# Causal mask matmuls on 64 by 64 tiles of the array: two heads in the rows, two halves of the keys in the columns

## The chip, the core and the metric

The kernel runs on one core of a Trainium2 chip. A core has a matrix engine (TensorE, in the profile PE for matmuls and PEld for weight loads), a vector engine (DVE), a scalar engine (ACT), GpSimd (POOL) and queues that start DMAs (SP among them). Matmuls read their operands from SBUF and write to PSUM[...]. The engines run side by side and wait for one another through semaphores.

The metric is device time in microseconds. Before the change it is 3176.01 us, the median of 3 runs (3175.93 to 3178.2).

## What is computed

A pre-norm block on x of shape 8 x 1024 x 512: an attention whose queries, keys and values are sines and cosines of the normalised input, and then a mixture of eight experts. What matters here is the causal attention:

```python
B, S, D = x.shape                       # 8, 1024, 512
H, dh = w_q.shape                       # 16, 32
...
Q = jnp.concatenate([cos_q, sin_q], axis=-1)      # 64 per head
...
K = jnp.concatenate([cos_k, sin_k], axis=-1)
...
V = cos_v + sin_v
scores = jnp.einsum('bqhd,bkhd->bhqk', Q, K) / scale
causal = jnp.triu(jnp.ones((S, S), dtype=bool), k=1)
scores = jnp.where(causal, -jnp.inf, scores)
attn = jax.nn.softmax(scores, axis=-1)
out = jnp.einsum('bhqk,bkhd->bqhd', attn, V).reshape(B, S, D)
```

A head's queries and keys have 64 elements each, so a product of them needs only half of the array's 128 rows.

## The kernel before

The attention stage goes through 32 steps (`n` in the main loop; 8 sequences times 4 groups of four heads). A step has two pairs of heads, and each pair two halves `h` of the queries (512 each): 128 passes of score tiles in all. The generator `scores` makes the tiles of one pass one after another, with keys in the partitions and queries in the columns. The two heads of a pair, `a` = 0 and 1, lie in partitions 0 to 63 and 64 to 127 of `pair` and so in the upper and lower 64 rows of the array, and they write to two banks of PSUM (`ps[:, a, ...]`). The score matmuls (L684, fp32) take a stationary operand of 64 rows by 128 keys, which the profile writes as "64*128". An fp32 matmul shows up as two passes, each with its own weight load, so that a score tile of 512 queries for two heads makes four rows in the trace.

Tiles in which no key is later than a query need no mask. In each pass three tiles hold the diagonal: one of 512 queries (a first block of 128 keys), one that puts two blocks of keys side by side (384 and 128 queries), and one of 256. There `scores` adds a large negative number to the scores of later keys, by matmuls in bf16 that accumulate into the same PSUM (L698). Their rows are not elements of a query but 64 keys of a half block: the stationary operand `keys_b` holds identity blocks, and the moving operand `later_b` holds 0 or the negative number for each of the 64 keys and each of up to 128 queries. `part` is the half of the 128 keys: half 0 needs only the first 64 queries, half 1 all 128. So a diagonal tile has four mask matmuls, two halves for two heads; in the tile with two key blocks, each covers both blocks in one instruction (128 and 256 columns instead of 64 and 128). Before the change `keys_b` has 128 columns for each half, of which the other half's 64 are zero, so that every mask matmul writes all 128 partitions of the tile and adds zero to the other half.

After its mask each tile goes to ACT, which takes the exponential of both heads at once (L704) out of PSUM into SBUF; three score tiles fit in PSUM (`ps_sc`, 3 buffers). `attend` then multiplies them with the values (AV, L718, fp32, stationary 128 keys by 64 columns, "128*64"), the two heads in the two halves of the columns. `by_halves` (L216) transposes with 64 rows by 128 columns. The router's matmuls (L858, L875) use tiles of 128 rows by 32 columns, the experts (L1238 and on) all of 128 by 128.

The order of the instructions on PE, ACT, DVE and SP is written by hand: the main loop (L1736 to L1899) advances the generators of scores, attention, transposes, layernorm and router in turn, and each engine carries out its instructions in that order. The stage ends where the last `attend` ends, and PE goes over to the experts. `mask` (L288), called once at the start (L1720), fills `later_b` and `keys_b` on POOL from the fp32 masks of `rest_of_loads`; L266 first clears `keys_b`.

Of the kernel before, what the change touches and what calls it, by code (L numbers as in the profile page):

```python
# [15 lines left out]
BF16 = mybir.dt.bfloat16  # L16
# [6 lines left out]
P = 128  # L23
# [51 lines left out]
def preln_attn_moe_kernel(  # L75
# [21 lines left out]
    nc = tc.nc  # L97
# [35 lines left out]
    own = to_router.pool("own", 1, **left)  # L133
# [48 lines left out]
    ident = own.tile([P, P], F32, name="ident")  # L182
# [26 lines left out]
    def two_banks():  # L209
        return ps_sc.tile([P, 2, 512], F32, name="ps_s")  # L210
# [40 lines left out]
    ps = two_banks()[:, 0, : 6 * NCH]  # L251
# [10 lines left out]
    before = own.tile([P, P], F32, name="before")  # L262


    keys_b = own.tile([P, 2, P], BF16, name="keys_b")
    nc.gpsimd.memset(keys_b, 0.0)  # L266
    later_b = own.tile([P, 2, P], BF16, name="later_b")
    e_row = own.tile([P, E], F32, name="e_row")
    e_row_low = own.tile([P, E], F32, name="e_row_low")
# [16 lines left out]
    later = row2.tile([P, NCH, 2 * P], F32, name="xT", bufs=1)[:, :3, :P]  # L286

    def mask():  # L288
        for part in range(2):
            for a in range(2):  # L290
                r = slice(a * 64, (a + 1) * 64)
                nc.gpsimd.tensor_copy(later_b[r, part, :], later[r, 1 + part - a, :])
                nc.gpsimd.tensor_copy(keys_b[r, part, part * 64 : part * 64 + 64], ident[r, r])

    def rest_of_loads():

# [367 lines left out]
    def tiles_of(h):  # L664


        def block(kb, at=0):
            q0 = max(512 * h, kb * P)
            return kb, q0, 512 * (h + 1) - q0, at

        d = 4 * h
        full = [[block(kb)] for kb in range(d + 1)]
        return full + [[block(d + 1), block(d + 3, 3 * P)], [block(d + 2)]]

    def scores(pair, h, es):

        for parts in tiles_of(h):
            n = sum(w for _, _, w, _ in parts)
            ps = two_banks()
            own_keys = parts[0][0] >= 4 * h  # L680
            for kb, q0, w, at in parts:
                for a in range(2):
                    r = slice(a * 64, (a + 1) * 64)
                    nc.tensor.matmul(  # L684
                        ps[:, a, at : at + w], lhsT=pair[r, 1, kb * P : (kb + 1) * P],
                        rhs=pair[r, 0, q0 : q0 + w], start=at == 0, stop=not own_keys,
                        skip_group_check=True,
                    )
            if own_keys:

                for part, w in ((0, 64), (1, P)):
                    for a in range(2):
                        r = slice(a * 64, (a + 1) * 64)
                        out_, late = ps[:, a, :w], later_b[r, part, :w]
                        if len(parts) == 2:
                            out_ = ps[:, a, :].rearrange("p (k q) -> p k q", q=P)[:, ::3, :w]
                            late = late.unsqueeze(1).to_broadcast([64, 2, w])
                        nc.tensor.matmul(  # L698
                            out_, lhsT=keys_b[r, part, :], rhs=late,
                            start=False, stop=part == 1, skip_group_check=True,  # L700
                        )

            e = ep.tile([P, 2, n], F32, name=f"e_{n}", bufs=8 if n == 512 else 2)
            nc.scalar.activation(  # L704
                e, ps[:, :, :n], AF.Exp, scale=UNIT * UNIT / math.sqrt(2 * DH)
            )
            es.append(e)
            yield
# [78 lines left out]
    def router(b):  # L787
# [163 lines left out]


        mask, prior = t3("mask"), t3("prior")
        TT(mask, hot[0], hot[1], ALU.add)
        nc.vector.memset(prior[:, 0, :], 0.0)
        for t in range(1, NTT):
            TT(prior[:, t, :], prior[:, t - 1, :], mask[:, t - 1, :], ALU.add)
        yield "places"
        place = one_bank()[:, : NTT * E]
        flat = lambda t: t.rearrange("p t e -> p (t e)")  # L960
        tokens_out(place, before, flat(mask), start=True, stop=False)
        tokens_out(place, ones, flat(prior), start=False, stop=True)
        place = place.rearrange("p (t e) -> p t e", e=E)
# [772 lines left out]
    for n in range(NCK):  # L1736
        more, late = n + 1 < NCK, last is not None
# [15 lines left out]
        if late:  # L1753
            products.insert(0, attend(n - 1, 1, 1, e11, halves1))
        ahead = [scores(pairs[0], h, es[h]) for h in range(2)]
        v_box = [None]
        asides = [keep(v_box, v_pre(n + 1))] if more else [first_rows]
# [94 lines left out]

        es, halves1 = [[], []], []
        ahead = [scores(pairs[1], h, es[h]) for h in range(2)]
        route_on(1)
        route_on(2)
# [103 lines left out]
```

## Time and profile before

| what | value |
|---|---|
| median of 3 runs | 3176.01 us (3175.93 to 3178.2) |
| the profiled execution, its own time | 3177.95 us |
| its span (first to last instruction) | 3176.2 us |
| mean granted clock of TensorE | 0.998 |
| mask matmuls L698: count, from, to | 1536, 36.4 us, 1251.3 us |
| their durations: 64, 128, 256 columns | 190, 217, 270 ns |
| exponentials L704 on ACT: count, busy, mean | 640, 569.4 us, 937 ns |
| casts of the masks on POOL (L292, L293), in all | 8, from 15.3 us to 17.3 us |

A row of the profile names a line of the kernel, an engine, an operation, what is written and read, and for a matmul the rows and columns of the stationary operand ("64*128") and the shape of the moving one ("64x512": 64 partitions, 512 columns). The duration of a matmul runs from its start until the end of its way through the array, which is modelled, so durations of matmuls that follow each other overlap. The time that one takes from the next is read from the distance of their starts.

### The profile page before, as it was taken

How to read it: one execution, taken by the hardware profiler on the slowest of the kernel's cores; microseconds unless marked ns; L12 is line 12 of the kernel's file. 1: busy time of each engine (PE TensorE's matmuls, PEld its weight loads, DVE VectorE, ACT ScalarE, POOL GpSimd, SP SyncE). 2: the span in 40 equal slices, each digit the busy share in tenths (PEclk: the TensorE clock that was granted, in tenths of full speed). 3: DMA queues.
4: the chain of work that ended last, by engine and by line, in shares of the span. 5: the costliest groups of instructions: out<-in, count | busy, mean ns of one | idle time of the engine just before them, and what ended most of it. 6: DMA issues, size and time to landing. Idle time of an engine off the chain costs nothing.

```text
span 3176.2 us, 52225 instructions
## 1 busy us (share of the span) xinstructions
PE 3112.0 (98%) x20086; PEld 2147.5 (68%) x20086; DVE 2303.7 (73%) x4808; ACT 1680.4 (53%) x2599; POOL 424.1 (13%) x387
## 2 busy tenths in 40 slices
PE   5999999999999999999999999999999999999998
PEld 2444444444444444689699699699698698698697
DVE  8888878887887775738658658658667767767765
ACT  7888888888888885413423423423423423423423
POOL 3000202020201122410110110110110110110010
PEclk9999999999999999999999999999999999999999
DMA  5535454555545352533523523523533433433421
GB/s 167 147 100 166 106 165 132 148 138 149 164 133 160 80 167 55 149 82 96 155 54 91 152 57 95 145 59 98 140 64 100 132 67 102 128 67 108 118 58 23
DMA packets 288552, 358.79 MB, mean 113 GB/s; under 512 B 28376, under 2 KB 199088, under 8 KB 276272
## 3 DMA queue, kind: packets, MB, share of 16 engines
q1 hardware_dynamic: 264944, 312.20, 33.7%
q0 software_dynamic: 22912, 43.22, 7.3%
q8 instruction: 160, 2.62, 0.4%
q14 instruction: 88, 0.72, 0.1%
q10 hardware_dynamic: 448, 0.02, 0.0%
HBM read 207.02 MB, written 81.22 MB: 91 GB/s over the span
## 4 chain that ended last, share of the span: by engine, by line
PE 78%; DVE 4%; ACT 1%; issue 1%; DMA 0%; SPq 0%; POOLq 0%; POOL 0%; DVEq 0%; ACTq 0%
PE ps_p L1238 30%; PE ps_p L1474 10%; PE ps_p L1537 10%; PE av L718 10%; PE ps_s L684 9%; PE ps_p L1352 8%; ACT e L704 1%; PE ps_s L216 1%; PE ps_s L698 1%; DVE qk_f L525 1%; DVE qk_r L448 0%; DMA qk<-qk_r 0%; DVE xT L838 0%; DVE xe L1174 0%; DVE xe_s L1186 0%
## 5 line engine op out<-in xcount | busy, mean ns | idle before, releaser
L704 ACT ACTIVATE e<-ps_s 128x1024 f32<-128x1024 f32 (+1 forms) x640 | 569.4, 937 | 183.5 <-PE ps_s L684 110.0
L684 PE MATMUL ps_s<-qk 64*128 64x512 f32 (+3 forms) x3072 | 598.3, 506 | 28.2 <-DMA qk<-qk_r 12.4
L718 PE MATMUL av<-e,v 128*64 128x512 f32 (+3 forms) x3072 | 523.4, 490 | 0.0
L684 PEld LDWEIGHTS ps_s<-qk 64*128 64x128 f32 x3072 | 262.3, 188 | 216.0 <-issue 106.9
L718 PEld LDWEIGHTS av<-e,v 128*64 128x64 f32 x3072 | 200.5, 137 | 283.0 <-issue 267.0
L1238 PE MATMUL ps_p<-xe,w 128*128 128x256 f32 (+1 forms) x1024 | 317.6, 433 | 1.1 <-issue 1.1
L1238 PE MATMUL ps_p<-xe_s,t 128*128 128x256 f32 (+1 forms) x1024 | 317.6, 433 | 0.0
L1238 PE MATMUL ps_p<-xe,t 128*128 128x256 f32 (+1 forms) x1024 | 317.6, 433 | 0.0
L1316 POOL DMA_INDIRECT out_dram<-y,slots x80 | 127.8, 1597 | 1261.3 <-ACT y L1311 1017.8
L769 POOL DMA_INDIRECT slot_d<-token,slot x128 | 156.6, 1223 | 997.3 <-issue 620.8
L1238 PEld LDWEIGHTS ps_p<-xe_s,t 128*128 128x128 f32 x1024 | 194.4, 190 | 81.4 <-issue 0.8
L1238 PEld LDWEIGHTS ps_p<-xe,t 128*128 128x128 f32 x1024 | 194.2, 190 | 80.4 <-issue 0.4
L1238 PEld LDWEIGHTS ps_p<-xe,w 128*128 128x128 f32 x1024 | 193.7, 190 | 79.4 <-issue 1.2
L1281 DVE TENSOR_TENSOR hid<-hid 128x256 f32<-128x256 f32 (+1 forms) x128 | 63.9, 499 | 206.4 <-ACT hid L1279 206.4
L1537 PE MATMUL ps_p<-w_t,hid 128*128 128x256 f32 x960 | 212.4, 379 | 0.8 <-DVE y L1590 0.8
L1537 PEld LDWEIGHTS ps_p<-w_t,hid 128*128 128x128 f32 x960 | 180.0, 190 | 24.4 <-DVE y L1590 1.2
L1238 PE MATMUL ps_p<-xe_s,w 128*128 128x256 f32 (+1 forms) x512 | 158.9, 433 | 0.6 <-ACT p L1254 0.6
L1352 PE MATMUL ps_p<-w,hid 128*128 128x256 f32 x640 | 142.9, 379 | 0.0
L1474 PE MATMUL ps_p<-w,hid 128*128 128x128 f32 x1104 | 141.8, 275 | 0.0
L698 PEld LDWEIGHTS <-keys_b 64*128 64x128 bf16 x1536 | 80.9, 95 | 89.7 <-issue 71.8
L1311 ACT ACTIVATE y<-y,slots 128x256 f32<-128x256 f32 (+1 forms) x120 | 65.9, 578 | 142.8 <-DVE y L1389 105.5
L1474 PEld LDWEIGHTS ps_p<-w,hid 128*128 128x128 f32 x1104 | 135.8, 192 | 2.3
(289 smaller groups left out, 5182.7 us busy)
## 6 DMA issues: line engine op xcount, KB each, us to landing
w<-in_L_ffn_W_dram SPq DMA_DIRECT2D x256, 256.0 KB, 3.4
w<-in_L_ffn_W_dram SPq DMA_DIRECT2D x64, 512.0 KB, 6.8
qk<-qk_c SPq DMA_DIRECT2D x124, 256.0 KB, 4.5
qk<-qk_r SPq DMA_DIRECT2D x120, 256.0 KB, 4.9
qk_base<-base_d SPq DMA_DIRECT2D x28, 1024.0 KB, 8.8
xn_d<-xn SPq DMA_DIRECT2D x72, 256.0 KB, 2.3
rows_d<-xg SPq DMA_DIRECT2D x70, 256.0 KB, 2.1
x_mid<-in_L_attn_x_dram SPq DMA_DIRECT2D x16, 1024.0 KB, 9.2
```

The source lines that it names most:

```text
L684: nc.tensor.matmul(ps[:, a, at : at + w], lhsT=pair[r, 1, kb * P : (kb + 1) * P], rhs=pair[r, 0, q0 : q0 + w], start=at == 0, stop=not own ...
L698: nc.tensor.matmul(out_, lhsT=keys_b[r, part, :], rhs=late, start=False, stop=part == 1, skip_group_check=True,)
L704: nc.scalar.activation(e, ps[:, :, :n], AF.Exp, scale=UNIT * UNIT / math.sqrt(2 * DH))
L718: nc.tensor.matmul(av[a * 64 : (a + 1) * 64, q0 - 512 * h :], lhsT=vt[:, kb, 2 * pr + a, :], rhs=es[i][:, a, at : at + w], start=kb == 0, ...
L769: queued = nc.gpsimd.indirect_dma_start(out=slot_d[b], out_offset=bass.IndirectOffsetOnAxis(ap=idx, axis=0), in_=src, in_offset=None,)
L1238: nc.tensor.matmul(ps, lhsT=weights[:, k, :], rhs=rows[:, k, :], start=first and k == 0, stop=last and k == 1, skip_group_check=True,)
L1281: TT(g1, g3, h22, ALU.add)
L1311: nc.scalar.activation(part, part, AF.Identity, scale=meta[:, e, jj[r], 1:2].bitcast(F32))
L1316: ins = nc.gpsimd.indirect_dma_start(out=out, out_offset=bass.IndirectOffsetOnAxis(ap=meta[:, e, jj[r], 0:1], axis=0), in_=y, in_offset=No ...
L1352: nc.tensor.matmul(ps, lhsT=hid[:, k, part, cols], rhs=ws[weight][:, k, :], start=first and k == 0, stop=last and k == NHQ - 1, skip_group ...
L1474: nc.tensor.matmul(ps, lhsT=left[:, k, :], rhs=right[:, k, :], start=first and k == 0, stop=k == 3, skip_group_check=True,)
L1537: nc.tensor.matmul(ps[:, b * DC : (b + 1) * DC], lhsT=hid[:, k, part, b * P : (b + 1) * P], rhs=ws[weight][:, k, :], start=first and k == ...
```

## The change

`keys_b` becomes a single 64 by 64 identity for each head's rows, without the zero columns, and each mask matmul writes only the 64 partitions of its own half of the keys. The four mask matmuls of a tile then use four different quarters of the array: the head sets the rows, the half of the keys sets the columns. Their number, order and moving operands stay as they are. The memset that cleared `keys_b` goes, and two of its four casts on POOL.

```diff
-    keys_b = own.tile([P, 2, P], BF16, name="keys_b")
-    nc.gpsimd.memset(keys_b, 0.0)
+    keys_b = own.tile([P, 64], BF16, name="keys_b")
...
     def mask():
-        for part in range(2):
-            for a in range(2):
-                r = slice(a * 64, (a + 1) * 64)
+        for a in range(2):
+            r = slice(a * 64, (a + 1) * 64)
+            for part in range(2):
                 nc.gpsimd.tensor_copy(later_b[r, part, :], later[r, 1 + part - a, :])
-                nc.gpsimd.tensor_copy(keys_b[r, part, part * 64 : part * 64 + 64], ident[r, r])
+            nc.gpsimd.tensor_copy(keys_b[r, :], ident[r, r])
...
                 for part, w in ((0, 64), (1, P)):
                     for a in range(2):
                         r = slice(a * 64, (a + 1) * 64)
-                        out_, late = ps[:, a, :w], later_b[r, part, :w]
+                        keys = ps[part * 64 : (part + 1) * 64, a, :]
+                        out_, late = keys[:, :w], later_b[r, part, :w]
                         if len(parts) == 2:
-                            out_ = ps[:, a, :].rearrange("p (k q) -> p k q", q=P)[:, ::3, :w]
+                            out_ = keys.rearrange("p (k q) -> p k q", q=P)[:, ::3, :w]
                             late = late.unsqueeze(1).to_broadcast([64, 2, w])
                         nc.tensor.matmul(
-                            out_, lhsT=keys_b[r, part, :], rhs=late,
-                            start=False, stop=part == 1, skip_group_check=True,
+                            out_, lhsT=keys_b[r, :], rhs=late, start=False, stop=True,
+                            skip_group_check=True,
                         )
```

## Prediction

> **What bounds the kernel now.** I read the page first, then the stretch of time in which the changed line runs, then the chain of waits and the waits of TensorE in that stretch, and last single matmuls in the timeline.
>
> ```profile
> span 3176.2 us, 52225 instructions
> ...
> PE 3112.0 (98%) x20086; PEld 2147.5 (68%) x20086; DVE 2303.7 (73%) x4808; ACT 1680.4 (53%) x2599; POOL 424.1 (13%) x387
> ...
> PE ps_p L1238 30%; PE ps_p L1474 10%; PE ps_p L1537 10%; PE av L718 10%; PE ps_s L684 9%; PE ps_p L1352 8%; ACT e L704 1%; PE ps_s L216 1%; PE ps_s L698 1%; DVE qk_f L525 1%; DVE qk_r L448 0%; DMA qk<-qk_r 0%; DVE xT L838 0%; DVE xe L1174 0%; DVE xe_s L1186 0%
> ```
>
> TensorE is busy 98% of the span and the chain that ends last is nearly all its own work; the mask's matmuls (L698) are 1% of it. They run between 35.8 and 1251.3 us. The next line is the stretch view of 30 to 1251 us (columns: stretch, its length, busy time of PE, PEld, DVE, ACT, POOL, clock, DMA):
>
> ```profile
> 30.00:1251.00 1221.00, 1198.32 (x10427) 593.89 (x10429) 979.61 (x1926) 1019.56 (x1027) 162.74 (x144) 1.00 0.48 137
> ```
>
> In the attention stage PE is busy 98%, ACT 84%, DVE 80%. So time added to PE there is added to the span, but for the places where PE now waits for ACT to free one of the three score tiles. The waits of 60 to 1250 us (total us, times, longest) say how much that is:
>
> ```profile
> PEld ps_s L684 <- ACT e L704: 27.3, 65, 3.9
> PEld ps_s L216 <- ACT e L704: 8.0, 23, 0.9
> ```
>
> About 35 us. After 1251 us the experts run on a PE that is full, so a delay is passed on whole.
>
> **How cheap the mask is today.** One pass of score tiles in the timeline, PE and its weight loads (start, busy, group):
>
> ```profile
> 601.30 1.02 PE L684 MATMUL ps_s<-qk 64*128 64x512 f32 x4
> 601.74 0.10 PEld L698 LDWEIGHTS <-keys_b 64*128 64x128 bf16 x2 [0.23 <-issue]
> 602.16 0.25 PE L698 MATMUL ps_s<-later_b,keys_b 64*128 64x64 bf16 x4
> ...
> 602.25 1.09 PE L684 MATMUL ps_s<-qk 64*128 64x384 f32 x8
> ...
> 603.17 0.33 PE L698 MATMUL ps_s<-later_b,keys_b 64*128 64x128 bf16 x4
> ...
> 603.34 0.60 PE L684 MATMUL ps_s<-qk 64*128 64x256 f32 x4
> ...
> 603.77 0.25 PE L698 MATMUL ps_s<-later_b,keys_b 64*128 64x64 bf16 x4
> 603.95 0.20 PEld L718 LDWEIGHTS av<-e,v 128*64 128x64 f32 x4
> 603.95 1.08 PE L718 MATMUL av<-e,v 128*64 128x512 f32 x4
> ```
>
> [...] Scores (L684) and mask (L698) both use the array as 64 rows by 128 columns ("64*128"). The mask's weights are loaded at 601.74, under the scores. A narrow mask block costs 0.085 us until the next scores start (602.16 to 602.25), a wide one 0.165 (603.17 to 603.34). But from the third block to AV (L718, "128*64") it is 0.18, not 0.085, and AV's weights are loaded only at its own start. That 0.095 is what a change of tile shape costs. A change of columns alone, which is what this edit makes, is in the router:
>
> ```profile
> 1281.55 0.81 PE L1238 MATMUL ps_p<-xe_s,t 128*128 128x384 f32 x2
> ...
> 1281.87 0.49 PE L1238 MATMUL ps_p<-xe_s,t 128*128 128x384 f32 x1
> 1282.29 0.42 PE L875 MATMUL ps_t<-xT,wr_sb 128*32 128x256 f32 x4
> ```
>
> Two matmuls of L1238 start 0.32 apart (1281.55, 1281.87), but the first of the 32-column tiles starts 0.42 later: again 0.10. All four column tiles of L875 run as one (busy 0.42, for one of them 0.40), so tiles of one shape do overlap, about 7 ns apart.
>
> **Price of the change.** By the program's order there are 384 mask blocks, all behind scores: 256 narrow (64 then 128 columns), 128 wide (twice that). Next in order: scores 284 times (127 narrow to L684 384, 94 wide to L684 256, 63 narrow to L684 512), AV 33, transposes (L216) 67.
>
> 1. Into 64*64: 384 x 0.098 = 37.6 us. [...]
> 2. Out of it: every block but those before AV, where a change is paid already: 351 x 0.098 = 34.4 us.
> 3. Weights that are no longer loaded under a matmul. The page's weight loads:
>
> ```profile
> L684 PEld LDWEIGHTS ps_s<-qk 64*128 64x128 f32 x3072 | 262.3, 188 | 216.0 <-issue 106.9
> L718 PEld LDWEIGHTS av<-e,v 128*64 128x64 f32 x3072 | 200.5, 137 | 283.0 <-issue 267.0
> ...
> L698 PEld LDWEIGHTS <-keys_b 64*128 64x128 bf16 x1536 | 80.9, 95 | 89.7 <-issue 71.8
> ```
>
> 188 - 137 = 51 ns for 64 columns, so 102 for 128. After a change the load stands bare. Behind AV:
>
> ```profile
> 642.56 1.13 PE L684 MATMUL ps_s<-qk 64*128 64x512 f32 x4
> 643.52 0.25 PE L698 MATMUL ps_s<-later_b,keys_b 64*128 64x64 bf16 x4
> ```
>
> 0.96 for two passes of 512 columns, against 0.86 from 601.30 to 602.16: 0.10. The mask's own load [...] is not in the trace (64 columns of bf16): between 26 ns, if bf16 takes half of fp32, and 51, the same width in L718's row. I take 51, since the quick 95 is a 128-column load [...]: 384 x 0.051 = 19.6 us (10.0 at the low end). The scores behind the mask: behind a narrow block they wait some 0.056 today (602.25 to 603.17 is 0.92 for the same columns as 0.86) and would wait 0.105: 190 x 0.049 = 9.3; behind a wide block nothing today (603.34 to 603.77 is two plain passes): 94 x 0.105 = 9.9. Transposes: 0 to 53 ns x 67, taken as 3.
> 4. What the packing saves. By form, L698 takes 190, 217 and 270 ns for 64, 128 and 256 columns, so 64 columns stream in 27 ns. Side by side, the short half lies under the long one, and the block ends three offsets of 7 ns after its first start: 72 instead of 85 ns narrow, 125 instead of 165 wide: 256 x 0.013 + 128 x 0.040 = -8.4 us. [...]
> 5. POOL loses one 0.30 us memset (L266) and two casts of 0.23; its mask work ends at 17.3 us, the first mask is at 36, and the first scores wait for a DMA: 0. No DMA, semaphore wait or order of instructions changes; keys_b is smaller, nothing else is placed anew.
>
> Sum: 37.6 + 34.4 + 19.6 + 19.2 + 3 - 8.4 = +105 us of PE.
>
> **What hides.** Of the 35 us that PE waits for ACT, a part is taken up by the added time. Once in most of the 32 steps the scores behind a step's third mask wait 0.2 us for ACT (630.65: "0.20 <-ACT e L704"), with mask blocks in front: 32 x 0.2 = 6.4, surely gone. For the rest, ACT itself starts later when the mask before it ends later, so I take a quarter, some 8. Hidden: 15, between 5 and 35. ACT gets no new work, and at 1020 busy us in a stage of 1310 it does not become the bound.
>
> **Forecast.** The profiled execution took 3177.95 (1.75 outside its span). 3177.95 + 105 - 15 = 3268; the median 3176.01 lies 1.9 below the profiled run, so 3266. Its own range: [...] no saving and 5 hidden give 105 + 8.4 - 5 = +108, 3284.
>
> **Rivals.**
> - *No drain between 64*128 and 64*64* [...]. Then only step 4 and a slightly less covered load behind narrow blocks (72 ns of cover instead of 85, 190 x 0.013 = 2.5) remain: -6, 3170. [...] Against it: every change of shape I find in this trace pays 0.095 to 0.10, in both directions, columns alone too (on the way back, L875 to L1238, 1282.53 to 1282.86: 0.33 for four tiles 7 ns apart of 256 columns, which take 0.21). 7%.
> - *A drain only one way* (narrowing or widening is free): one of steps 1 and 2 goes with the bare load behind it, some 57 us: 105 - 57 - 15 = +33, 3209. Against it the router rows in both directions. 4%.
> - *The halves do not run together:* each of the second half's loads follows the first's matmul. Saving lost (+8.4) and 384 x 0.051 more: +118, 3294. For: no 64*64 tile with two rows and two columns at once is in the trace. Against: L718's pairs and L875's fours. 11%.
> - *Each of the four tiles drains:* 384 x 0.098 more on that: 3332. 4%.
> - The main case: 74%.
>
> The range 3230 to 3300 holds the main case and the third rival. Three runs differ by 2.3 us, so 0.2% (6.4 us) is about the least that can be told from no change. Slower by more: main case, both dearer rivals and the one-way drain, 93%; the no-drain case sits at the bound and is split, 4% same, 3% faster.
>
> **What would show it.** In the profile after: narrow block to next scores 0.32 instead of 0.085, wide 0.37 instead of 0.165; "64*64" in L698's form; its loads starting with the matmul instead of under the scores; two passes of 512 behind a mask 0.96; PE waits for ACT below 35 us; attention ending near 1340, and everything after unchanged in length. Wrong would be a gap into or out of the mask as short as today's, or a second gap inside the block.

## The result and the profile after

| | before | after |
|---|---|---|
| median | 3176.53 us (3175.93 to 3178.2, 4 runs) | 3246.83 us (3246.57 to 3247.05, 4 runs) |
| profiled execution, its span | 3177.95, 3176.2 | 3247.02, 3245.3 |

The change makes the kernel slower by 70.3 us, a ratio of 1.022 (95% interval 1.0203 to 1.0238). First the row of the exponentials (L704) as it was before, then the page after:

```profile
L704 ACT ACTIVATE e<-ps_s 128x1024 f32<-128x1024 f32 (+1 forms) x640 | 569.4, 937 | 183.5 <-PE ps_s L684 110.0
```

```profile
span 3245.3 us, 52222 instructions
...
PE 3188.3 (98%) x20086; PEld 2140.1 (66%) x20086; DVE 2305.1 (71%) x4808; ACT 1686.2 (52%) x2599; POOL 429.2 (13%) x384
...
L704 ACT ACTIVATE e<-ps_s 128x1024 f32<-128x1024 f32 (+1 forms) x640 | 573.9, 937 | 252.4 <-PE ps_s L698 135.7
...
L698 PEld LDWEIGHTS <-keys_b 64*64 64x64 bf16 x1536 | 43.4, 103 | 156.1 <-issue 140.8
```

PE's busy time grew by 76 us and no other engine's by more than 6. ACT's exponentials do what they did, but wait longer (252 us in all instead of 184), and now mostly for the mask (L698). The scores are line 683 here, one line earlier than before. All of the growth lies in attention. Its last AV group starts 69.1 us later, and the span is 69.1 us longer, so the experts behind it take as long as before. Before and after:

```profile
1251.49 5.81 PE L718 MATMUL av<-e,v 128*64 128x512 f32 x32
```

```profile
1320.58 5.81 PE L718 MATMUL av<-e,v 128*64 128x512 f32 x32
```

The timeline after, PE and its weight loads, around two narrow blocks (the first rows) and one wide block:

```profile
600.69 0.60 PE L683 MATMUL ps_s<-qk 64*128 64x512 f32 x2
601.21 0.11 PEld L698 LDWEIGHTS <-keys_b 64*64 64x64 bf16 x4 [0.76 <-issue]
601.22 0.25 PE L698 MATMUL ps_s<-later_b,keys_b 64*64 64x64 bf16 x4
...
601.40 1.14 PE L683 MATMUL ps_s<-qk 64*128 64x384 f32 x8
602.46 0.30 PE L698 MATMUL ps_s<-later_b,keys_b 64*64 64x128 bf16 x4
602.70 0.70 PE L683 MATMUL ps_s<-qk 64*128 64x256 f32 x4
603.33 0.25 PE L698 MATMUL ps_s<-later_b,keys_b 64*64 64x64 bf16 x4
603.51 1.99 PE L683 MATMUL ps_s<-qk 64*128 64x512 f32 x8
```

Read the starts again. The last pass of 512 columns starts at 600.69 and the mask at 601.22: 0.53, where a pass takes 0.43 (before, two of them took 0.86), so **0.10 on the way in**. The prediction's rivals call such a gap a drain; what the array does in it no trace shows. The weight loads start with the matmul (601.21) and not under the scores. From the first mask matmul to the next scores it is 0.18 (601.22 to 601.40; 603.33 to 603.51), and for the wide block 0.23 (602.46 to 602.70, to the nanosecond 0.232). With the way in, a narrow block costs 0.28 instead of 0.085 and a wide one 0.33 instead of 0.165. The scores behind the narrow block take 1.07 (601.40 to 602.46, to the nanosecond 1.067) where they took 0.92 (602.25 to 603.17 before). Of the 0.15 more, 0.10 is the way into the next mask and 0.05 a load laid bare.

The packing itself works. The four matmuls of the first narrow block start at 601.215, 601.219, 601.222 and 601.225, and they are over in 0.25, where one alone takes 0.24. Before, the second half of the keys started 0.028 behind the first (602.164 and 602.192). The durations of L698 in its line's view (shortest, median, longest in ns):

```profile
L698 PE MATMUL ps_s<-later_b,keys_b x1536: 212/240/420, 37.5 to 1320.4; 64*64 64x64 bf16 x128, 64*64 64x128 bf16 x64
```

The shortest and the median were 188 and 217. I read the 24 ns more as the mask's own load, which the matmul now waits for: a bare load of 128 fp32 columns lengthens a score matmul in the same way (512 columns from 0.59 to 0.69). And PE's waits for ACT between 60 and 1320 us:

```profile
PEld ps_s L683 <- ACT e L704: 11.5, 34, 2.8
PEld ps_s L216 <- ACT e L704: 6.8, 17, 0.9
```

Together 18 us, where they were 35. So some 17 us of the added time went into waits that were there before. PE's idle time, up to the first matmul of the experts, fell by only 7 us (stretch, length, then PE busy; before and after):

```profile
30.00:1259.74 1229.74, 1205.48 (x10481) 596.98 (x10482) 981.37 (x1930) 1021.20 (x1029) 168.46 (x151) 1.00 0.48 136
```

```profile
30.00:1328.83 1298.83, 1281.82 (x10481) 587.37 (x10482) 982.05 (x1930) 1026.48 (x1029) 175.20 (x152) 1.00 0.45 129
```

The two do not contradict each other: while PE waits, the matmul before the wait is still on its way (0.59 us long, 0.43 from start to start), and by these modelled durations that part of the wait counts as busy.

### The profile page after: what moved, and what is told of

Its sections match the earlier page's. It is cut to its first block, busy times and chain, and to the rows that moved or that the text cites. A ratio compares the mean times of both kernels' runs of the same rounds, so it can differ in the third digit from the quotient of the medians.

```text
span 3245.3 us, 52222 instructions
## 1 busy us (share of the span) xinstructions
PE 3188.3 (98%) x20086; PEld 2140.1 (66%) x20086; DVE 2305.1 (71%) x4808; ACT 1686.2 (52%) x2599; POOL 429.2 (13%) x384
## 4 chain that ended last, share of the span: by engine, by line
PE 92%; DVE 5%; ACT 1%; issue 1%; DMA 1%; SPq 0%; POOLq 0%; POOL 0%; DVEq 0%; ACTq 0%
PE ps_p L1238 30%; PE ps_s L683 16%; PE av L718 15%; PE ps_p L1474 10%; PE ps_p L1537 9%; PE ps_p L1352 7%; PE ps_s L698 2%; PE ps_s L216 2%; DVE qk_f L524 1%; DVE qk_r L447 1%; DMA xn<-in_L_attn_x_dram 0%; DVE xT L838 0%; PE ps_s L875 0%; DVE v L447 0%; PE ps_s L858 0%
## 5 line engine op out<-in xcount | busy, mean ns | idle before, releaser
L704 ACT ACTIVATE e<-ps_s 128x1024 f32<-128x1024 f32 (+1 forms) x640 | 573.9, 937 | 252.4 <-PE ps_s L698 135.7
L683 PE MATMUL ps_s<-qk 64*128 64x512 f32 (+3 forms) x3072 | 625.4, 516 | 21.8 <-DMA qk<-qk_r 12.4
L1537 PEld LDWEIGHTS ps_p<-w_t,hid 128*128 128x128 f32 x960 | 180.4, 190 | 24.1 <-DVE y L1590 1.2
L698 PEld LDWEIGHTS <-keys_b 64*64 64x64 bf16 x1536 | 43.4, 103 | 156.1 <-issue 140.8
L726 DVE TENSOR_SCALAR av_sb<-av,inv_o 128x512 f32<-128x512 f32 x128 | 95.4, 745 | 66.7 <-PE av L718 66.7
```

The costliest lines, as they stand in the source:

```text
L683: nc.tensor.matmul(ps[:, a, at : at + w], lhsT=pair[r, 1, kb * P : (kb + 1) * P], rhs=pair[r, 0, q0 : q0 + w], start=at == 0, stop=not own ...
L698: nc.tensor.matmul(out_, lhsT=keys_b[r, :], rhs=late, start=False, stop=True, skip_group_check=True,)
L704: nc.scalar.activation(e, ps[:, :, :n], AF.Exp, scale=UNIT * UNIT / math.sqrt(2 * DH))
L726: nc.vector.tensor_scalar(av_sb, av, inv_o[:, q : q + 1], None, ALU.mult)
L1537: nc.tensor.matmul(ps[:, b * DC : (b + 1) * DC], lhsT=hid[:, k, part, b * P : (b + 1) * P], rhs=ws[weight][:, k, :], start=first and k == ...
```

## The experiments

Eight kernels ran in two groups. Each group has runs of the kernel before on its own chip, and a rise is counted from these alone. Their median is 3191.81 us for the two kernels with an extra matmul and the two with POOL, and 3177.16 for the other four.

**An extra matmul, with and without a change of shape.** To the kernel before, one matmul with zero weights is added behind each mask block, on 64 moving columns; the two kernels differ in the columns of its weights alone (64 or 128).

```diff
+                nc.tensor.matmul(
+                    ps[:64, 0, :64], lhsT=nothing_b[:64, :64], rhs=later_b[:64, 0, :64],
+                    start=False, stop=True, skip_group_check=True,
+                )
```

With 64 columns:

> The kernel before with one more matmul behind each of the 384 mask blocks: zero weights of 64 rows by 64 columns on 64 moving columns, so that the array changes its shape to 64*64 and back and nothing is gained by packing. Theory: 384 x (0.097 in + 0.024 load + 0.027 columns) + 351 x 0.097 out + bare loads behind it 190 x 0.049 + 94 x 0.105 + 67 x 0.05, 113 us of PE, less 20 to 30 hidden: 3260 to 3270. Rival (a change of shape costs nothing by itself, the packed block with its four loads does): 10 us of columns, 3180 to 3190.

With 128 columns (`ps[:P, ...]`, `nothing_b[:64, :P]`):

> The same extra matmul with zero weights of 64 rows by 128 columns, in the shape that scores and mask have already. Theory: no drain; 384 x 0.027 of columns, and the scores' load has only its 27 ns as cover instead of 57 or 109: 190 x 0.03 + 94 x 0.08, 23 us of PE, less 5 to 12 hidden: 3188 to 3196. Rival (any further matmul with its own load costs as much as the 64*64 one): 3260.

Measured: 3282.12 with 64 columns, +90.3 us (ratio 1.0282, 1.0264 to 1.0299), and 3212.22 with 128, +20.4 (1.0062, 1.0045 to 1.0078). As rises over before, the theory's expectations were +83 to +93 and +11 to +19; the second is just exceeded. One instruction, half as wide, costs 70 us more, 0.18 for each of 384 places, though it packs nothing and saves nothing. So the price is the change of shape, with the loads that it lays bare, and not the four small tiles or their four loads. The first of the two in the timeline of PE:

```profile
610.76 0.25 PE L700 MATMUL ps_s<-later_b,keys_b 64*128 64x64 bf16 x4
610.94 0.21 PE L704 MATMUL ps_s<-later_b,nothing_b 64*64 64x64 bf16 x1
611.08 1.14 PE L686 MATMUL ps_s<-qk 64*128 64x384 f32 x8
```

and of the second:

```profile
600.08 0.25 PE L700 MATMUL ps_s<-later_b,keys_b 64*128 64x64 bf16 x4
600.17 0.19 PE L704 MATMUL ps_s<-later_b,nothing_b 64*128 64x64 bf16 x1
600.17 1.13 PE L686 MATMUL ps_s<-qk 64*128 64x384 f32 x8
```

The mask (L700) is the old one in both. In the second kernel the extra matmul starts 0.09 behind it and the scores at the same rounded time; in the first it starts after 0.18 and the scores 0.14 later again. The parts give about that: 0.097 for the way out, a load of 0.024 and 0.027 of columns, 0.148.

**Packing only one kind of tile.** Both kernels keep the padded weights of before, and pack where the condition holds.

```diff
+                packed = len(parts) == 2
...
+                        keys = ps[half, a, :] if packed else ps[:, a, :]
...
+                            out_, lhsT=keys_b[r, part, half] if packed else keys_b[r, part, :],
```

> Packed on 64x64 only in the tile with two key blocks (128 of 384 blocks), the others as before. Theory by the gaps seen in the changed kernel: 94 blocks before scores at 0.097 + 0.097 + 0.024 + 0.105 - 0.053 = 0.27 and 34 before transposes at 0.215, 33 us of PE, less 5 to 15 that PE's waits for ACT take up: 3195 to 3204. If this middle block is hidden by ACT's backlog wholly: 3177 to 3185. If packing itself paid where it saves most (0.053 a block) and the change of shape were free: 3170.

> Packed on 64x64 only in the two tiles with one key block (256 blocks), the wide one as before. Theory: the rest of the sum of 90 us of PE, 57, less 8 to 15 hidden: 3218 to 3226, and with the wide-only kernel's rise together 65 to 75 us if the hidden time is split between them. If each of the two alone hides the same waits: the two rises together come to 50 to 60 only.

Measured: 3201.26 for the wide tiles alone (+24.1, ratio 1.0073, 1.0056 to 1.009) and 3218.64 for the narrow ones (+41.5, 1.013, 1.0113 to 1.0147). Both lie where the sum of gaps put them, and together they make 65.6 of the 70.3 of both. Even the wide block, where packing saves twice as much, loses. The hidden part is split between the two for the most part. If the same waits were hidden twice, the rises would come to 50 to 60. The idle time of PE says the same: up to the experts it fell by 3.3 us with the wide tiles packed, by 5.0 with the narrow ones, and by 7.3 with both.

**Half as many changes, by masking two tiles together.** The packed masks of the first two diagonal tiles are put behind the scores of the second.

```diff
+            held.append((ps, n, parts))
+            if parts[0][0] == 4 * h:
+                continue
...
+            for _ in held:
+                yield
```

> The changed kernel with one edit: the first two diagonal tiles of each pass are scored one behind the other, then masked together on 64x64 tiles, then exponentiated. The packed mask matmuls and their loads are the same 1536, but one way in and one way out of the 64x64 shape goes at 127 places. Theory (the change of shape and the loads it lays bare are the price): each place saves 0.097 in, 0.097 out, 0.024 of the mask's own load and 0.105 of the next scores' load, 0.32 in all, 41 us of PE; with PE waits for ACT coming back in part, 3206 to 3228. Rival (the packed block itself is dear, by its loads or its small tiles): the same blocks, so 3247, or more since ACT gets the first tile 0.9 us later.

Measured: 3278.48, a ratio to before of 1.0317 (1.0299 to 1.0334), some 31 us worse than the change. The expected time was missed, and the trace says in which half of the reasoning. The shared block of eight mask matmuls, here before transposes, and the stretch up to the experts:

```profile
637.40 0.36 PE L703 MATMUL ps_s<-later_b,keys_b 64*64 64x64 bf16 x8
637.69 0.71 PE L216 MATMUL ps_s<-ident,av_sb 64*128 64x64 f32 x16
```

```profile
30.00:1359.89 1329.89, 1254.34 (x10481) 590.82 (x10482) 984.49 (x1930) 1011.39 (x1029) 164.26 (x152) 1.00 0.44 126
```

The shared block takes 0.29 from its first start to the next shape (637.40 to 637.69), where a narrow and a wide block took 0.18 and 0.23 and one more way in of 0.10. With the load of 0.105 that the middle scores no longer wait for, that is the expected 0.32 a place. PE's busy time fell by 27 us (the sum said 41; new waits count in part as busy, as above), but its idle time rose from 17 to 76. Two score tiles are now held at once of the three buffers (`ps_sc`), which the transposes use too (L762 empties theirs), and ACT gets the first one later. In this kernel the waits of PE between 60 and 1350 us are led by these:

```profile
PEld ps_s L684 <- ACT e L709: 44.1, 105, 3.6
PE ps_s L684 <- DVE o_p L762: 36.4, 31, 1.2
PEld ps_s L216 <- ACT e L709: 22.0, 55, 0.9
```

So fewer changes do cost PE less, but the waits for a free buffer take more than that. The time alone would have spoken for the rival. That more score buffers would turn this into a gain is not shown.

**No mask on TensorE.** What can any cheaper mask gain?

```diff
-            if own_keys:
-
-                for part, w in ((0, 64), (1, P)):
...
```

> The kernel before without the mask matmuls: later keys are not masked, so this part of the computation is left out. It prices all that any mask on TensorE can save. By the gaps of before: 256 x 0.085 + 128 x 0.165 = 43 us of PE and 190 x 0.056 = 11 of loads laid bare, 54 in all; PE then waits more for ACT, by 5 to 25: 3128 to 3148. Rival (the mask was already hidden behind ACT): 3165 to 3176.

Measured: 3149.24, -27.9 us (ratio 0.9911, 0.9895 to 0.9928), 1 us above the upper end of the range. So about half of the 54 us counted by gaps did not come out as time. The waits of the scores for ACT (line L690 in this kernel), summed over matmuls and weight loads, grow from 32 to 79 us; part of them runs while matmuls are still on their way.

```profile
PEld ps_s L684 <- ACT e L690: 65.9, 143, 4.6
PE ps_s L684 <- ACT e L690: 13.2, 35, 4.4
```

**The mask on POOL.** That pointed to a version that might beat both kernels: POOL, which is busy 13% of the time, sets the later keys to zero behind the exponential.

```diff
+            if own_keys:
+                for _, _, _, at in parts:
+                    own_q = e[:, :, at : at + P]
+                    nc.gpsimd.affine_select(
+                        out=own_q, in_=own_q, compare_op=ALU.is_ge, fill=0.0, base=0,
+                        pattern=[[0, 2], [1, P]], channel_multiplier=-1,
+                    )
```

> No mask on TensorE; POOL zeroes the later keys of the four diagonal blocks of each pass in the exponentials in SBUF (512 selects of 128 x 256). PE is freed as in the kernel without a mask, 3149; the selects [...] stand between ACT and AV. If AV comes late enough behind ACT: 3149 to 3160, faster than both kernels. If POOL's queue, in which the router's scatters stand, holds the selects up[...]: above 3177.

The second kernel does this for the wide tile alone (`if len(parts) == 2`) and leaves the other masks on TensorE:

> Only the wide tile's mask is moved to POOL (256 selects), the narrow ones stay on TensorE as before. PE loses 128 x 0.165 = 21 us and the loads behind the wide blocks are bare by 94 x 0.105 = 10 instead: 11 us of PE, less what PE waits more for ACT (half of it in the kernel without a mask): 3165 to 3173. If POOL's queue holds AV up: above 3177.

Measured: 3317.4 (ratio 1.04, 1.0383 to 1.0418) and 3285.52 (1.0298, 1.0281 to 1.0315), slower than before by 125.6 and 93.7 us. Two waits of the first kernel between 60 and 1390 us, and a part of POOL's timeline:

```profile
PEld av L711 <- POOL e L696: 133.7, 151, 4.7
PE av L711 <- POOL e L696: 74.3, 37, 4.6
```

```profile
335.47 2.25 POOL L696 TENSOR_SCALAR_AFFINE_SELECT e<-e 128x256 f32<-128x256 f32 x3
341.16 1.16 POOL L762 DMA_INDIRECT slot_d<-token,slot  x1 [3.45 <-DMA slot_d<-token,slot]
342.35 0.41 POOL L696 TENSOR_SCALAR_AFFINE_SELECT e<-e 128x256 f32<-128x256 f32 x1
```

The median select takes 0.41 us (the mean 0.63; what lengthens the others is open), but in POOL's timeline a scatter of the router that waits 3.45 us for the one before it to land stands in front of this one. AV waits for the select. The two rows of waits overlap, so they are not to be added: 74.3 us is what AV's matmuls waited, in 37 waits, and in 24 of them, 66 us, POOL spent more than half of the wait on a scatter or on a landing. That the selects would be harmless without the scatters is not shown: another order of POOL's queue was not tried.

Waiting is not the whole price. Up to the experts, without a mask and with the mask on POOL (two chips):

```profile
30.00:1230.22 1200.22, 1166.78 (x8945) 547.87 (x8946) 979.56 (x1930) 1005.34 (x1029) 176.89 (x151) 1.00 0.49 139
```

```profile
30.00:1384.20 1354.20, 1208.88 (x8945) 556.60 (x8946) 999.63 (x1930) 1006.51 (x1029) 451.62 (x652) 0.97 0.43 124
```

PE has the same 8945 matmuls, but it is busy 42 us longer with them, beside 112 us more of idle time, and its granted clock (the number before the last two) is 0.97 instead of 1.00. The last section shows two places where the clock falls. How much of the 42 us is the clock, and how much the ends of matmuls before new waits, is not separated.

## Why the prediction was right, and where it was too high

The direction, the mechanism and the place were as forecast; 3266 was forecast and 3246.8 measured, a rise of 70 instead of 90, inside the range. The misses are of size and nearly all lie on one side, so no large error made up for another.

- **Steps 1 and 2, the way in and out.** Forecast 0.098 at 735 places, 72 us. Measured 0.097 on the way in (the median over the blocks is 0.096 to 0.097), and the way out fits the same figure: 71 us. The pair of extra matmuls shows that the price comes with the change of shape. The rival in which the change is free, and the one in which it is free in one direction, fall with it. So do the price at each of the four tiles and halves that do not overlap: the four matmuls of a block start within 0.010 us (601.215 to 601.225), with no gap between them. With both ways, a narrow block came to 0.28 and a wide one to 0.33, where 0.32 and 0.37 were forecast; the mask's own load and the saving, below, make the difference.
- **Step 3, the mask's own load.** Forecast 51 ns, an estimate from the fp32 load of the same width; measured 24, close to the low end (26) that half of fp32 gave. 384 x 0.024 = 9.2 us instead of 19.6. This is the largest miss, 10.4 us, and it is the term taken from a row of another type. The narrow load is indeed the slower one in its own row (103 ns for 64 columns, 95 for 128 before), but that did not make it as long as an fp32 load (137 for 64 columns).
- **Step 3, bare loads behind the mask.** Forecast 19.2 and 3. The scores of 384 queries behind a narrow block grew by 0.049, as forecast, those behind a wide block by 0.102 (0.105 was forecast), and the transposes by 0.051 at 67 places, 3.4 us. But the 0.056 of cover lost today was read at one block and taken for all 190. At 42 of the 63 blocks with 512 queries behind them the load was bare already, at most of them because it waited for ACT to free a buffer, as in the first block below (before). There the term was nothing, 2.1 us in all.

```profile
630.34 0.25 PE L698 MATMUL ps_s<-later_b,keys_b 64*128 64x64 bf16 x4
630.65 0.30 PEld L684 LDWEIGHTS ps_s<-qk 64*128 64x128 f32 x4 [0.20 <-ACT e L704]
```

```profile
664.62 0.25 PE L698 MATMUL ps_s<-later_b,keys_b 64*64 64x64 bf16 x4
664.79 0.30 PEld L683 LDWEIGHTS ps_s<-qk 64*128 64x128 f32 x4
```

- **Step 4, the saving.** Forecast 8.4, from tiles 7 ns apart. The four matmuls start 3 to 4 ns apart: a narrow block's own part is 0.180 - 0.097 - 0.024 = 0.059 instead of 0.085, a wide one's 0.233 - 0.121 = 0.112 instead of 0.165 (the starts to the nanosecond). 256 x 0.026 + 128 x 0.053 = 13.4 us, so 5.0 less cost. The 7 ns came from the router's four column tiles, which are of another shape (128*32).
- **The hidden part.** With these terms the sum is 37.2 + 34.0 + 9.2 + 17.1 + 3.4 - 13.4 = 87.5 us of PE. 70.3 measured leaves 17 hidden, where 15 was forecast; the two waits for ACT fell by 17 too. Some 10 of them lie where the forecast looked, at the 63 blocks with 512 queries behind them. The pair above is one: 0.31 from mask to scores before, with a wait of 0.20, and 0.18 after, with none. Over the 63 this distance fell by 3.8 us in sum, where the way out and the block alone would have added 6.0. Where the rest lies is open.

10.4 + 5.0 + 2.1 + some 2 are the 20 us between forecast and result. The memset and the casts on POOL were put at nothing; PE's first transposes start 0.33 us earlier (18.94 instead of 19.27), which is the most that they can be worth.

## What to carry to other kernels

Look at the shapes of the neighbours before packing matmuls into quarters of the array. Each switch of shape cost 0.097 us here, and it laid bare a load on either side; a block that saves 0.03 to 0.05 cannot pay for two of them. One added matmul in the shape of its neighbours cost 0.05 a place, and in a shape of its own 0.24. Price a change by the distances of starts at places where the old kernel already does what the new one will do more often, and ask how much of what PE gains would only become a wait for the next engine: here, without any mask, about half did.

## What the runs showed of the hardware

Tiles of one shape that use different rows and columns started 3 to 4 ns apart (601.215 to 601.225 for four), against 6 to 7 for two tiles on different rows before (602.164 and 602.170, 602.192 and 602.199). And in two waits of AV for POOL the granted clock of TensorE fell from 1.00 to 0.50. In the kernel with the whole mask on POOL, PE's timeline shows a wait of 4.25 us before AV and then one of 3.45, and the stretch view (the number before the last two is the granted clock) shows the clock beside them:

```profile
336.07 3.29 PE L711 MATMUL av<-e,v 128*64 128x512 f32 x12 [4.25 <-POOL e L696]
342.81 1.12 PE L711 MATMUL av<-e,v 128*64 128x256 f32 x4 [3.45 <-POOL e L696]
```

```profile
335.42:338.83 3.41, 2.76 (x8) 0.96 (x10) 2.97 (x4) 0.00 (x0) 2.28 (x4) 0.50 0.90 288
338.83:342.25 3.42, 0.53 (x6) 0.14 (x2) 2.64 (x9) 0.00 (x0) 1.09 (x1) 1.00 0.18 70
342.25:349.07 6.82, 6.26 (x16) 2.51 (x18) 5.02 (x9) 2.05 (x2) 2.65 (x5) 0.50 0.01 0
349.07:360.00 10.93, 10.93 (x64) 4.42 (x62) 3.61 (x17) 10.00 (x12) 5.43 (x8) 1.00 0.02 2
```

The granted clock fell to 0.50 at 335.42 and 342.25, 0.65 and 0.56 us before the waits ended, and it stayed there for 3.4 us the first time and 6.8 us the second, while PE worked. In the second stretch the weight loads of the scores show what a pass of 512 columns took:

```profile
345.74 0.34 PEld L684 LDWEIGHTS ps_s<-qk 64*128 64x128 f32 x2 [0.51 <-issue]
...
346.59 0.34 PEld L684 LDWEIGHTS ps_s<-qk 64*128 64x128 f32 x2 [0.51 <-issue]
...
347.44 0.34 PEld L684 LDWEIGHTS ps_s<-qk 64*128 64x128 f32 x2 [0.51 <-issue]
```

They start 0.85 apart, where a pass took 0.43 at a clock of 1.00 (before, 600.45 to 600.88). So the second stall cost more than its own length. What makes the clock fall is not shown.
